# Weighted sums of two attention layers by Strassen's scheme, in groups of two query blocks, with the values projected ahead

## The chip, the core and the metric

The kernel runs on one core of a Trainium2 chip. Five engines work beside each other and meet at semaphores: TensorE (PE in the profile, with its weight loads shown as PEld), VectorE (DVE), ScalarE (ACT), GpSimd (POOL) and SyncE (SP), whose queue issues most of the DMAs; POOL issues the others. The metric is the device time of one execution in microseconds (us).

## What is computed

A stack of four graph layers works on 2708 nodes with 512 features each and one adjacency matrix of 2708 x 2708. After each layer, x becomes the layer norm of x plus the layer's output. The change touches the last two layers, which are attention over all nodes, in fp32:

```python
def _L2_gnn_ref(x, adj, weight, bias, node_w, edge_w):
    node_att = jax.nn.softmax(x @ node_w, axis=0)
    h = x @ edge_w
    e = h @ h.T
    e = jnp.where(adj > 0, e, NEG_BIG)
    edge_att = jax.nn.softmax(e, axis=1)
    combined_att = node_att * edge_att
    support = x @ weight
    output = adj * combined_att @ support
    return output + bias

def _L3_gnn_ref(x, adj_matrix, spatial_matrix, Wq, bq, Wk, bk, Wv, bv):
    query = x @ Wq + bq
    key = x @ Wk + bk
    value = x @ Wv + bv
    scale = 1.0 / jnp.sqrt(jnp.asarray(query.shape[-1], dtype=query.dtype))
    a = query @ key.T * scale
    a = a + adj_matrix + spatial_matrix
    attn = jax.nn.softmax(a, axis=-1)
    return attn @ value
```

In layer 2 the scores `h @ h.T` are symmetric. In layer 3 `adj_matrix` and `spatial_matrix` are both the adjacency. Each layer has two large products: scores (queries by keys) and weighted sums (exponentials by values).

## The kernel before

The nodes are cut into 22 blocks of 128 rows (`BLOCKS`). The last has only 20. A block of queries by a block of keys is a tile of 128 x 128 scores.

Queries are taken in groups of three blocks (`GROUPS`, L1176 to L1182), seven groups, of which the last has four blocks, the short one among them. Keys are taken one block at a time. `softmax_layer` (L1216) builds both layers and returns two functions, and the loop at the end of the kernel calls them: step `t` of `score_step` makes the scores of one key block for one group (`one_score`, L1285), and `sum_step` runs `lag = NT + AHEAD` = 25 steps behind it. So while one group is scored, the one before it is summed. Layer 3's scoring starts 12 steps after layer 2's ends, beside layer 2's last sums.

`one_score` loads the adjacency tile of the step (`load_a`, five buffers), multiplies keys by queries over four chunks of 128 features (L1303), and `score` combines the result with the adjacency: in layer 2 ACT turns the adjacency into a mask (L1650) and DVE applies it (L1651), in layer 3 DVE adds twice the adjacency (L1735). DVE keeps a running maximum (L1351). In layer 2 a score block whose transpose has been made is not made again: the raw scores are copied (L1340), stored in DRAM by POOL, loaded back for the later group and transposed on TensorE (L1295). `key_order` mixes such mirrored steps with the others within a group. The short key block's four feature chunks run packed side by side, and a matmul with `quarters` adds them up (L1337).

When a group is scored, `spread_max` turns its maximum into a row that stands on all partitions (`nmax`). `one_exp`, one step ahead of the sums, subtracts it (DVE, L1401), takes the exponential (ACT, L1402), adds to the row sums (DVE, L1408), and in layer 2 multiplies by a second load of the adjacency (DVE, L1654).

`one_sum` is the weighted sum (L1424). In layer 2 the exponentials of a query block are the weights of the array and 512 value columns stream past, one PSUM bank for each query block, and the four banks are handed round from group to group. In layer 3 the rows of x take the place of the values, and the result is a transposed sum in four banks, one for each 128 features. `end` copies these to SBUF, and `project` multiplies them by `Wv` afterwards (L1532).

`end` also makes the row sums' reciprocals (L1474, L1484). `finish2` scales and adds x (L1660), and later pieces of work, kept in the list `later`, do the layer norm and transpose the new x into the keys of layer 3 (L1195). The loop takes a piece off that list only on odd steps, and none on the last of a group. Layer 3 uses the space of layer 2's values (`sup`) for queries, weights and results.

The order of instructions on an engine follows the program except where a build-time scheduler puts a later instruction in front of one that it takes to be waiting.

Of the kernel before, what the change touches and what calls it, by code (L numbers as in the profile page):

```python
# [29 lines left out]
def gnn_stack_kernel(  # L30
# [1145 lines left out]
    GROUP = 3  # L1176
    lonely = NT % GROUP == 1
    GROUPS = [list(range(g, min(g + GROUP, NT))) for g in range(0, NT - lonely, GROUP)]
    if lonely:
        GROUPS[-1].append(NT - 1)  # L1180
    GSPAN = [(g[0] * P, sum(BLOCKS[it][1] for it in g)) for g in GROUPS]
    GW = max(w for _, w in GSPAN)  # L1182
    GB = max(len(g) for g in GROUPS)

# [5 lines left out]
    def transpose_block(psum, dst, it, copy):  # L1190

        n = BLOCKS[it][1]
        tp = psum.tile([P, C, P], F32, tag="tp", name="tp")
        for c in range(C):
            nc.tensor.transpose(  # L1195
                tp[:, c, :n], xs[:n, it, c * P : (c + 1) * P], ident[:n, :n]
            )
        copy(dst, tp[:, :, :n])
# [15 lines left out]
    AHEAD = 3  # L1214

    def softmax_layer(  # L1216
        att, psum, later, keys, values, query, score, weigh, finish, after=None, sums=None
    ):

        mirror = after is None
        HOME = {it: gi for gi, group in enumerate(GROUPS) for it in group}

        def key_order(gi):

            late = list(range(NFULL // 2)) + [NT - 1] + list(range(NFULL // 2, NFULL))
            if not mirror:

                return late if gi else list(range(NFULL - 1)) + [NT - 1, NFULL - 1]
            early = [jt for jt in late if HOME[jt] < gi]
            late = [jt for jt in late if HOME[jt] >= gi]
            place = {jt: (k + 0.5) / len(early) for k, jt in enumerate(early)}
            place |= {jt: (k + 0.5) / len(late) for k, jt in enumerate(late)}
            return sorted(place, key=place.get)

        kept = {
            (g, gi): dram.tile([GSPAN[gi][1], GSPAN[g][1]], F32, name=f"scores_{g}_{gi}")
            for gi in range(len(GROUPS) if mirror else 0)
# [3 lines left out]
        values4 = []  # L1247

        def last_values():

            t = att.tile([P, F], F32, tag="values4", name="values4", bufs=1)
            for c in range(C):
                nc.gpsimd.dma_start(t[c * Q : c * Q + REST], values[:REST, NT - 1, :])
            values4.append(t)

        def load_a(gi, jt):
            c0, w = GSPAN[gi]
            j0, m = BLOCKS[jt]
            a = att.tile([P, GW], F32, tag="a", name="a_cols", bufs=5)
            if m < P:  # L1260
                nc.vector.memset(a, 0.0)
            for r in range(0, P, P if m == P else Q):
                nc.sync.dma_start(a[r : r + m, :w], adjT[j0 : j0 + m, c0 : c0 + w])
            return a

        def load_kept(gi, jt):

            g = HOME[jt]
            src = kept[g, gi][:, j_in(jt)]
            s = att.tile([P, GB, P], F32, tag="sm", name="s_kept", bufs=3)  # L1270
            full = sum(BLOCKS[it][1] == P for it in GROUPS[gi])
            nc.sync.dma_start(
                s[:, :full, :], src[: full * P].rearrange("(b p) j -> p b j", p=P)
            )
            for b in range(full, len(GROUPS[gi])):
                n = BLOCKS[GROUPS[gi][b]][1]
                nc.sync.dma_start(s[:n, b, :], src[b * P : b * P + n])
            return s

        def j_in(jt):  # L1280

            b = jt - GROUPS[HOME[jt]][0]
            return slice(b * P, b * P + BLOCKS[jt][1])

        def one_score(st, k):  # L1285
            gi, jt = st["gi"], st["order"][k]
            c0, w = GSPAN[gi]
            j0, m = BLOCKS[jt]
            a = load_a(gi, jt)
            ps = psum.tile([P, BANK], F32, tag="ps_s", name="ps_s")  # L1290
            if mirror and HOME[jt] < gi:
                s = load_kept(gi, jt)
                for b, it in enumerate(GROUPS[gi]):
                    n = BLOCKS[it][1]
                    nc.tensor.transpose(  # L1295
                        ps[:, b * P : b * P + n], s[:n, b, :], ident[:n, :n]
                    )
            elif m == P:

                own = mirror and HOME[jt] == gi  # L1300
                b = jt - GROUPS[gi][0] if own else 0
                for c in range(C):
                    nc.tensor.matmul(  # L1303
                        ps[:, b * P : w],
                        keys[:, c, j0 : j0 + P],
                        st["q"][:, c, b * P :],
                        start=(c == 0),
                        stop=(c == C - 1),
                    )
                for o in range(b):  # L1310
                    nc.tensor.transpose(
                        ps[:, o * P : (o + 1) * P],
                        st["own"][o][:, (b - o - 1) * P : (b - o) * P],
                        ident,
                    )
                after_own = (GROUP - b - 1) * P if own else 0
                if after_own:
                    s = att.tile([P, GROUP * P], F32, tag="sraw", name="s_own", bufs=3)
                    nc.scalar.copy(
                        s[:, :after_own], ps[:, (b + 1) * P : (b + 1) * P + after_own]  # L1320
                    )
                    st.setdefault("own", []).append(s)
            else:

                parts = psum.tile([P, BANK], F32, tag="tp", name="ps_parts")
                for c in range(C):
                    nc.tensor.matmul(
                        parts[c * Q : (c + 1) * Q, :w],
                        keys[:, c, j0 : j0 + Q],
                        st["q"][:, c, :],  # L1330
                        start=True,
                        stop=True,
                    )
            e = att.tile([P, GW], F32, tag="e", name="e", bufs=NT + AHEAD + 2)
            if m < P:
                nc.scalar.copy(e[:, :w], parts[:, :w])
                nc.tensor.matmul(ps[:, :w], quarters, e[:, :w], start=True, stop=True)  # L1337
            if mirror and HOME[jt] > gi:
                s = att.tile([P, GROUP * P], F32, tag="sraw", name="s_raw", bufs=3)
                nc.scalar.copy(s[:m, :w], ps[:m, :w])  # L1340
                nc.gpsimd.dma_start(kept[gi, HOME[jt]][j_in(jt), :], s[:m, :w])
# [54 lines left out]
        def one_exp(st, k):  # L1396
# [12 lines left out]
            if weigh:  # L1409
                weigh(e, load_a(gi, jt)[:, :w])  # L1410
# [229 lines left out]
    with (  # L1640
# [41 lines left out]
        def room(first, blocks, *shape):  # L1682
# [3 lines left out]
            for d in shape:  # L1686
                size *= d
# [171 lines left out]
```

## Time and profile before

| what | value |
|---|---|
| median of 3 runs | 3232.13 us (3231.83 to 3232.38) |
| profiled execution, first to last instruction | 3228.0 us |
| layer 2's projections begin to end | about 1465 to 1613 us |
| attention of layers 2 and 3 | about 1613 to 3218 us |
| granted TensorE clock | 0.999 |
| mean DMA rate over the span | 122 GB/s |

The page of a profile lists, for groups of instructions, the line of the kernel, the engine, what is written and read, how many there were, their busy time and mean duration, and what they waited for. An fp32 matmul shows as two records, so that a count of 882 is 441 matmuls. The chain follows the work that ended last back from the end. Busy times of matmuls are partly modelled, so that the distance between starts says more than a mean duration. These groups of the page are of use below:

```profile
L1303 PE MATMUL ps_s<-sup,hT 128*128 128x384 f32 (+1 forms) x1176 | 407.5, 490 | 0.0
L1424 PE MATMUL po<-sup,e 128*128 128x512 f32 x882 | 407.0, 595 | 0.0
L1424 PE MATMUL po<-e,xs 128*128 128x384 f32 (+1 forms) x1176 | 406.1, 489 | 0.0
```

The first is layer 3's scores, the second layer 2's sums, the third layer 3's sums.

### The profile page before, as it was taken

Reading aid. Unit: us, or ns where it says so; the run is one execution under the profiler, and the core shown is the slowest. Engines: PE = TensorE matmul, PEld = TensorE weight load, DVE = VectorE, ACT = ScalarE, POOL = GpSimd, SP = SyncE. Lnnn points to the kernel's source line nnn. Section 1 sums busy time; section 2 is a strip of 40 time slices with the busy share of each in tenths; the row PEclk is TensorE's granted clock in tenths of the full one; section 3 lists DMA queues with packets and bytes.
Section 4 is the critical chain, followed back from the end, with each engine's and each line's share of the span. In section 5 each row is a group of like instructions: output and inputs, shape, how many; then the busy total and the mean of one; then the engine's idle time right before and its main releaser. Section 6 shows DMA issues by size and latency. Waiting matters only on the chain.

```text
span 3228.0 us, 30366 instructions
## 1 busy us (share of the span) xinstructions
PE 3194.0 (99%) x10882; PEld 1714.7 (53%) x10882; DVE 1933.6 (60%) x3166; ACT 1327.7 (41%) x1505; POOL 134.9 (4%) x218
## 2 busy tenths in 40 slices
PE   8999999999999999999999999999999999999999
PEld 5444444544444447875555555554555555555554
DVE  7889987776786784444154677776344342542533
ACT  6898896477867461001142434442011020120211
POOL 1100100000000000000010000000000000000000
PEclk9999999999999999999999999999999999999999
DMA  7867865156546314540054444553211111111100
GB/s 276 307 230 244 292 236 196 45 183 210 182 167 211 139 58 125 143 107 1 0 155 119 129 133 139 146 161 93 75 43 32 44 34 38 43 30 46 34 24 20
DMA packets 175125, 394.81 MB, mean 122 GB/s; under 512 B 21210, under 2 KB 116390, under 8 KB 169150
## 3 DMA queue, kind: packets, MB, share of 16 engines
q1 hardware_dynamic: 158326, 312.84, 32.0%
q0 software_dynamic: 16208, 77.93, 6.3%
q8 instruction: 85, 1.39, 0.2%
q10 hardware_dynamic: 440, 2.10, 0.2%
q14 instruction: 66, 0.54, 0.1%
HBM read 312.69 MB, written 78.52 MB: 121 GB/s over the span
## 4 chain that ended last, share of the span: by engine, by line
PE 79%; DVE 8%; issue 7%; ACT 3%; DMA 2%; POOL 0%; SPq 0%; DVEq 0%; POOLq 0%; ACTq 0%
PE po L1424 24%; PE ps_s L1303 18%; PE po L504 11%; PE ps_nb L1156 7%; PE ps_wide L1205 5%; DVE t L416 3%; PE ps_sup L1601 2%; PE ps_mlp L792 2%; PE ps_o L1532 2%; PE ps_hid L128 2%; ACT t L417 2%; PE ps_dec L923 2%; DVE a L397 1%; ACT t L408 1%; PE ps_s L1295 1%
## 5 line engine op out<-in xcount | busy, mean ns | idle before, releaser
L416 DVE SCALAR_TENSOR_TENSOR t<-t,a 128x2708 f32<-128x2708 f32 (+1 forms) x152 | 450.1, 2974 | 145.3 <-ACT t L408 140.3
L408 ACT ACTIVATE t<-f1b,f2h 128x1354 f32<-128x1354 f32 (+1 forms) x304 | 415.6, 1412 | 44.0 <-PE po L504 34.3
L417 ACT ACTIVATE t<-t 128x2708 f32<-128x2708 f32 (+1 forms) x152 | 373.1, 2456 | 101.5 <-DVE t L416 101.3
L504 PE MATMUL po<-t,xw 128*128 128x452 f32 (+3 forms) x1056 | 407.6, 549 | 4.9 <-ACT t L417 4.4
L1303 PE MATMUL ps_s<-sup,hT 128*128 128x384 f32 (+1 forms) x1176 | 407.5, 490 | 0.0
L1424 PE MATMUL po<-sup,e 128*128 128x512 f32 x882 | 407.0, 595 | 0.0
L1424 PE MATMUL po<-e,xs 128*128 128x384 f32 (+1 forms) x1176 | 406.1, 489 | 0.0
L504 PE MATMUL po<-t,emb 128*128 128x452 f32 (+3 forms) x1056 | 397.7, 545 | 4.0 <-ACT t L417 3.7
L1735 DVE SCALAR_TENSOR_TENSOR e<-a_cols,ps_s 128x384 f32<-128x384 f32 (+1 forms) x154 | 85.5, 555 | 449.2 <-PE ps_s L1303 426.3
L1303 PEld LDWEIGHTS ps_s<-sup,hT 128*128 128x128 f32 x1176 | 221.9, 190 | 164.1 <-issue 14.3
L1424 PEld LDWEIGHTS po<-e,xs 128*128 128x128 f32 x1176 | 222.4, 190 | 160.1 <-issue 6.1
L504 PEld LDWEIGHTS po<-t,xw 128*128 128x128 f32 (+1 forms) x1056 | 188.6, 189 | 212.3 <-issue 191.7
L504 PEld LDWEIGHTS po<-t,emb 128*128 128x128 f32 (+1 forms) x1056 | 193.7, 190 | 201.1 <-issue 189.7
L1424 PEld LDWEIGHTS po<-sup,e 128*128 128x128 f32 x882 | 160.5, 190 | 159.2 <-issue 137.0
L1303 PE MATMUL ps_s<-hT 128*128 128x384 f32 (+5 forms) x672 | 211.1, 461 | 0.9 <-ACT sup L1608 0.7
L1402 ACT ACTIVATE e<-e 128x384 f32<-128x384 f32 (+1 forms) x308 | 151.7, 522 | 117.7 <-DVE e L1401 114.6
L1156 PE MATMUL ps_nb<-hid_hi,at 128*128 128x512 f32 x484 | 185.7, 391 | 0.4 <-DVE at L1148 0.4
L1650 ACT ACTIVATE a_cols<-a_cols,neg_big 128x384 f32<-128x384 f32 (+1 forms) x154 | 94.7, 616 | 219.2 <-DMA a_cols<-in_adjT_dram 183.0
L1156 PE MATMUL ps_nb<-hid_lo,at 128*128 128x512 f32 x462 | 180.2, 390 | 0.0
L108 ACT ACTIVATE ln_rstd<-ln_rstd 128x1 f32<-128x1 f32 (+1 forms) x88 | 17.3, 201 | 389.8 <-DVE ln_rstd L107 389.1
L1401 DVE TENSOR_TENSOR e<-e,nmax 128x384 f32<-128x384 f32 (+1 forms) x308 | 162.6, 550 | 23.3 <-ACT nmax L1394 23.3
L1303 PEld LDWEIGHTS ps_s<-hT 128*128 128x128 f32 x672 | 123.2, 190 | 89.3 <-issue 19.6
(252 smaller groups left out, 3317.7 us busy)
## 6 DMA issues: line engine op xcount, KB each, us to landing
a<-adj_d SPq DMA_DIRECT2D x108, 677.0 KB
a_cols<-in_adjT_dram SPq DMA_DIRECT2D x378, 192.0 KB
a<-in_adjT_dram SPq DMA_DIRECT2D x42, 677.0 KB
adj_d<-a POOLq DMA_DIRECT2D x42, 677.0 KB, 5.9
kept<-t POOLq DMA_DIRECT2D x20, 1354.0 KB, 6.7
t<-kept SPq DMA_DIRECT2D x20, 1354.0 KB
raw<-in_adjT_dram SPq DMA_DIRECT2D x105, 256.0 KB
a_cols<-in_adjT_dram SPq DMA_DIRECT2D x63, 202.0 KB
```

The lines of the kernel that those rows point to most:

```text
L408: tanh = nc.scalar.activation(tv[:, k, :], f1b[k][:n, :w], AF.Tanh, bias=f2h[:n, jt, h : h + 1], scale=0.5,)
L416: step = nc.vector.scalar_tensor_tensor(tv, tv, GUARD, ab, ALU.add, ALU.mult)
L417: exp = nc.scalar.activation(tv, tv, AF.Exp, scale=0.5)
L504: nc.tensor.matmul(po[HB * k + q][:, :qw], values[r : r + n, jt, h * P : (h + 1) * P], t[r : r + n, k, q0 : q0 + qw], start=(place == 0), ...
L1156: nc.tensor.matmul(pos[it][:n], at, half[:, jt, :], start=(jt == 0 and k == 0), stop=(jt == NT - 1),)
L1205: nc.tensor.matmul(ps[:, :width], w(c, o), xt(c), start=(c == 0), stop=(c == C - 1),)
L1303: nc.tensor.matmul(ps[:, b * P : w], keys[:, c, j0 : j0 + P], st["q"][:, c, b * P :], start=(c == 0), stop=(c == C - 1),)
L1401: nc.vector.tensor_tensor(e, e, st["nmax"][:, :w], ALU.add)
L1402: nc.scalar.activation(e, e, AF.Exp)
L1424: nc.tensor.matmul(out, lhsT, rhs, start=(k == 0), stop=(k == NT - 1))
L1650: nc.scalar.activation(a, a, AF.Identity, bias=neg_big[: a.shape[0]], scale=1.0e30)
L1735: nc.vector.scalar_tensor_tensor(e, a, 2.0, ps, ALU.mult, ALU.add)
```

## The change

Queries are taken in groups of two blocks, eleven groups, and keys too: a step is now two query blocks by two key blocks. The last group of both kinds (`REMNANT`) has a full block and the short one. For a pair of full groups, the four products of 2 x 2 blocks (each split into two halves of 256 value columns, so eight of 256 columns) become seven, by Strassen's scheme in Winograd's form. It needs combinations of the values (`S`, and one block of `sup` overwritten), which are made once for each key group, combinations of the exponentials (`T`), which DVE makes in each step, and additions of the seven sums at the end of a group.

In layer 3, the values are projected ahead: layer 2's `later` work multiplies each new block of x by `Wv` and stores it in DRAM. While layer 2's last group is summed, `reload` brings these values into the space of layer 2's values. Rows of x no longer stay in SBUF: they are stored (`x2_d`, `x3_d`) and loaded for each group, and the space they had holds combinations and weights.

The parts of the diff that the text speaks of:

```diff
-    GROUP = 3
+    GROUP = 2
+    GROUPS = [[g, g + 1] for g in range(0, NT, GROUP)]
...
+            a = att.tile([P, GROUP, GW], F32, tag="a", name="a_cols", bufs=4)
+            ps = psum.tile([P, GROUP, GW], F32, tag="ps_s", name="ps_s")
+            e = att.tile([P, GROUP, GW], F32, tag="e", name="e", bufs=LAG + 2)
...
+        def end_exp(st, k):
...
+                    q = e.rearrange("p j (i c) -> p (j i) c", c=P)
+                    sub = lambda d, x, y: nc.vector.tensor_tensor(d, x, y, ALU.subtract)
+                    sub(t[:, 0:2, :], q[:, 1:4:2, :], q[:, 0:2, :])
+                    sub(t[:, 2, :], q[:, 3, :], t[:, 0, :])
+                    sub(t[:, 3, :], q[:, 2, :], t[:, 2, :])
...
+        def row_sums(st):
...
+                for jb in range(GROUP):
+                    nc.tensor.matmul(
+                        pr[:n, b : b + 1],
+                        st["acc"][:, jb, b * P : b * P + n],
+                        ones[:, 0:1],
...
+        def one_sum(st, k):
...
+            product(0, 0, e[:, 0, i1], v0[:, :HF])
+            product(0, 1, e[:, 1, i1], v1[:, :HF])
+            product(2, 0, t[:, 1, :], S[:, g, 2, :])
+            product(2, 1, t[:, 0, :], S[:, g, 0, :])
+            product(1, 0, t[:, 2, :], S[:, g, 1, :])
+            product(1, 1, t[:, 3, :], v1[:, HF:])
+            product(3, 0, e[:, 1, i2], v0[:, HF:])
...
+        def end(st):
...
+                add = lambda d, x, y: nc.vector.tensor_tensor(d, x, y, ALU.add)
+                nc.scalar.copy(at[0][0], po[0][:, 0, :])
+                add(at[1][1], at[0][0], po[1][:, 0, :])
+                add(at[0][0], at[0][0], po[0][:, 1, :])
+                add(at[0][1], at[1][1], po[2][:, 0, :])
+                add(at[1][0], at[1][1], po[2][:, 1, :])
+                add(at[1][1], at[0][1], po[2][:, 1, :])
+                add(at[0][1], at[0][1], po[1][:, 1, :])
+                add(at[1][0], at[1][0], po[3][:, 0, :])
...
+                later.extend(finish(it, parts[b][:n], rs[:n, b : b + 1], r[:n, b, :]))
...
+        def step(t, lag):
+
+            front = t + 1 - lag
+            early = front % NG != 0
+            if early:
+                exp_step(front, begin_exp)
+            if 0 <= t < total:
+                score_step(t)
+            if not early:
+                exp_step(front, begin_exp)
+            exp_step(front, end_exp)
+            if 0 <= t - lag < total:
+                sum_step(t - lag)
+            if 0 <= t < total:
+                score_end(t)
...
+    LAG = NG + 1
...
+        po = [
+            psum.tile([P, GROUP, HF], F32, tag=f"po{b}", name="po", bufs=1) for b in range(4)
+        ]
...
+        def combine(g):
...
+            tt(S[:, g, 0, :], b12, b22, ALU.add)
+            tt(S[:, g, 2, :], b11, b12, ALU.subtract)
+            tt(S[:, g, 1, :], S[:, g, 0, :], b11, ALU.subtract)
+            tt(b12, b21, S[:, g, 1, :], ALU.subtract)
...
+            def project():
+                ps = psum.tile([P, F], F32, tag="tp", name="ps_v")
+                project_rows(ps, hT[:, :, i0 : i0 + n], wv_sb, n)
+                v = att.tile([P, F], F32, tag="T", name="v3", bufs=2)
+                nc.scalar.copy(v[:n], ps[:n])
+                nc.gpsimd.dma_start(v3_d[i0 : i0 + n], v[:n])
+                nc.gpsimd.tensor_tensor(y, y, bv_sb[:n], ALU.add)
+                nc.gpsimd.dma_start(x3_d[i0 : i0 + n], y)
+
+            return [norm, project]
...
+        start3 = steps + 5
+        last2 = steps + LAG - 1
+        nc.sync.dma_start(wv_sb, wv.rearrange("(c p) o -> p c o", p=P))
...
+        for t in range(start3 + steps + LAG):
...
+            if t < steps + LAG:
+                step2(t, LAG)
+            if t >= start3:
+                step3(t - start3, LAG)
...
+            k = t - (last2 - NG + 1)
+            if 0 <= k < NG and order2(REMNANT)[k] != REMNANT:
+                reload(order2(REMNANT)[k])
+            if 2 <= k < NG + 2:
+                g = order2(REMNANT)[k - 2]
+                if g != REMNANT:
+                    combine(g)
-            if later and (k is None or (k % 2 and k < NT - 1)):
+            if later:
                 later.pop(0)()
```

`NG` is the number of groups, 11, and `HF` half of the 512 value columns. `step` runs one step of scores, the exponentials of the step that is summed next, and one step of sums, `LAG` = 12 steps behind the scores. All groups use the same four banks `po`. Where the short key group or the short query group takes part, the plain four products stay, with the 20 rows packed in four quarters of the array. The row sums now come before the last step's products. The list `later` gives up one piece in every step, from the step in which it was filled.

## The prediction

> **What bounds the kernel now.** I read the page's busy line and its chain first, then the chain in order of time and TensorE's timeline in layers 2 and 3, then the windows of layer 2, then VectorE's groups kept apart by shape.
>
> ```profile
> PE 3194.0 (99%) x10882; PEld 1714.7 (53%) x10882; DVE 1933.6 (60%) x3166; ACT 1327.7 (41%) x1505; POOL 134.9 (4%) x218
> ...
> PE po L1424 24%; PE ps_s L1303 18%; PE po L504 11%; PE ps_nb L1156 7%; PE ps_wide L1205 5%; DVE t L416 3%; PE ps_sup L1601 2%; PE ps_mlp L792 2%; PE ps_o L1532 2%; PE ps_hid L128 2%; ACT t L417 2%; PE ps_dec L923 2%; DVE a L397 1%; ACT t L408 1%; PE ps_s L1295 1%
> ```
>
> TensorE (PE) is busy 99% of the span, and the weighted sums (L1424) are the largest entry of the chain, 24%. A busy PE need not be at its peak, so I take spacing. Two stretches of the chain, then TensorE's timeline (start, duration, records):
>
> ```profile
> 2015.10 2.58 PE po L1424 x6
> 2017.67 2.58 PE ps_s L1303 x8
> ...
> 2369.39 2.58 PE ps_s L1303 x8
> 2371.97 2.58 PE po L1424 x8
> ```
> ```profile
> 2053.62 1.02 PE L1424 MATMUL po<-sup,e 128*128 128x512 f32 x2
> 2054.48 0.81 PE L1303 MATMUL ps_s<-hT 128*128 128x384 f32 x2
> 2055.13 1.88 PE L1424 MATMUL po<-sup,e 128*128 128x512 f32 x4
> ...
> 2067.63 1.89 PE L1303 MATMUL ps_s<-hT 128*128 128x256 f32 x8
> 2069.36 0.27 PE L1311 MATMUL ps_s<-ident,s_own 128*128 128x128 f32 x1
> ```
>
> Each fp32 matmul leaves two records. Three 512-wide products take 2.58 us, four 384-wide ones take 2.58: both 0.43 us for each 256 columns. Four 256-wide matmuls with four different weights take 2069.36-2067.63 = 1.73 us, again 0.43 each. So time goes by columns, without a penalty at 256. The first three lines of the timeline also show that the order on the engine is not the program's: at a group's end scores stand between the products of one step, while VectorE still empties banks.
>
> The reserve of VectorE (DVE) decides the rest. Windows of layer 2, then its groups there:
>
> ```profile
> 1780.00:1880.00 100.00, 100.00 (x319) 51.40 (x318) 63.68 (x144) 41.19 (x76) 7.51 (x14) 1.00 0.43 122
> 1880.00:1980.00 100.00, 100.00 (x326) 52.04 (x324) 71.32 (x166) 38.16 (x73) 5.38 (x10) 1.00 0.47 135
> 1980.00:2080.00 100.00, 99.27 (x330) 51.40 (x328) 76.42 (x172) 48.26 (x87) 3.76 (x7) 1.00 0.52 149
> 2080.00:2200.00 120.00, 120.00 (x396) 60.94 (x395) 88.36 (x192) 45.05 (x79) 1.62 (x3) 1.00 0.58 165
> ```
> ```profile
> L1654 DVE TENSOR_TENSOR e<-e,a_cols 128x384 f32<-128x384 f32 x132 | 72.9, 552 | 82.6 <-DMA a_cols<-in_adjT_dram 82.2
> L1651 DVE SCALAR_TENSOR_TENSOR e<-a_cols,ps_s 128x384 f32<-128x384 f32 x132 | 72.3, 549 | 80.0 <-ACT s_raw L1340 58.2 <-PE ps_s L1295 14.2 <-ACT s_own L1319 7.0
> L1401 DVE TENSOR_TENSOR e<-e,nmax 128x384 f32<-128x384 f32 x132 | 69.8, 546 | 8.5 <-ACT nmax L1394 8.5
> ```
>
> The columns of a window are its length, then PE, PEld, DVE, ACT and POOL busy, clock, DMA share, GB/s. PE has no gap worth naming, DVE climbs from 64% to 76%, as later groups mirror more scores and PE's step shortens. Most of DVE's idle time there is waiting, for adjacency tiles and for the raw copies: DVE is not yet late.
>
> [...] weight loads of 190 ns stand beside matmuls without adding to the 0.43 us. [...] Back to back, the trace starts 384-wide operations 0.468 us apart, 400 ns of columns and 68 fixed. From that spacing my estimates are 0.60 us for 512 columns, 0.34 for 256, 0.20 for 128. [...]
>
> **The change, part by part (PE).** Removed in layer 2: 21x21 full products, 147 steps of 2.58 us = 379; seven packed products of the short key block at 1.06 = 7; the short query block 5.5; its sum 1. Together 393. In layer 3: 126 steps of 2.58 = 325, 21 wider ones of 2.71 (404 columns) = 57, short keys 6, projections after the sums (L1532) 21x3.43 = 72, short rows 2. Together 462. Sum 855.
>
> Added, in each layer: 100 pairs of full groups with seven 256-wide products at 0.43 = 301. The short key group costs four products and one packed set, 1.72+0.56 = 2.3, ten times 23. The short query group the same, 23. Corner and picking matmuls 4.5. Together 351, twice 702. Values projected ahead: 22x3.43 = 75. Sum 777. PE gains 78.
>
> Given back: row sums take two one-column matmuls a block instead of one, at 0.19 us each (six records in 0.56): 22x2x0.19 = 8. Eleven sets of packed scores instead of seven: about 1. Score columns, transposed blocks and query columns stay as many, only cut at 256 instead of 384. Net PE: -68 us.
>
> **DVE and its cover.** In layer 2 a step of four blocks costs five 512-wide operations (mask, maximum, shift, row sum, adjacency), 3.0 us, and the new differences 0.34+2x0.20 = 0.74: 3.74, where 3 blocks cost 2.34 before. Eleven steps: 41. Per group come seven bank additions (2.5), finish (2.1), norms (3.4), maximum (1.1), memsets (0.6), and some 2 us of unavoidable waiting from the group's maximum to its first exponential: 53 us. PE in the group that sums gi and scores g=gi+1: 32.5 for sums, 2.7 for its own scores, 3.44x(9-g) for others, 0.44xg for mirrored ones, 1.2 short keys, 7.9 projections and transposes, 1.5 row sums and maxima. That is 59 at gi=5, 56 at 6, 53 at 7, 50 at 8, 47 at 9 (where DVE's narrow scores leave it 48). So DVE's work is hidden until gi=6 and late from gi=7: 0.3+3.3+1.2 = 5 us. [...] I add 3 us for each of five groups, 15. Loss 20. Ends: 0 if the projections, which now lie in this stage, cover all; 60 at 12 us for each of five groups. In layer 3 a step costs DVE 2.4+0.74 = 3.2 us against PE's 6.4: hidden.
>
> ACT: mask, exponential and raw copy at 512 columns stay below 2.2 us a step, plus two table loads a block: below PE everywhere, nothing. DMA: same bytes of adjacency and kept scores, in rows of 1 KB. The rows of x, the values and the reload add about 25 MB over 1600 us, while the share stands at 0.58 at most. On SP the adjacency loads queue behind the load of rows and of the kept scores, with four tiles of 256 KB where there were five of 192: about the same reach of two steps. I cost it at nothing. If that cover fails, the adjacency multiply on DVE is late, inside the 60.
>
> Between layers four steps have only the narrow sums, 2.2 us of PE each, beside DVE's exponentials, reloaded combinations (4x0.34) and norms, about 3 to 3.5 us. POOL's reloads wait for the PE step that frees the block, with value writes queued behind them. Loss 6, from 0 (query projections fill it) to 15. At the start SP's weight loads wait for the last stores of x, ahead of the first adjacency load: 3, from 0 to 5. At the end copy and picking replace projection: 1.
>
> Sum on the profiled execution: 3228.0-68+20+6+3+1 = 3190. The median stands 4.1 us above that span: **3194**.
>
> **The rivals.** First, DVE friction: bank additions, norms and differences hold each of layer 2's last five groups 8 us longer, as DVE runs at over 95%: 3194+35 = 3229. For it: 76% now, and 60% more DVE time a step for a third more blocks. Against: PE did not lose 1 us at 76%, and 75 us of projections move in.
>
> Second, the other side: **group ends stall PE**. All four banks are now owned by one group, and the first norm's transposes are put right after the group's end. They wait for a copy (0.37), seven additions (2.5), reciprocals and finish (2.1), then statistics, square root with table load and scaling (3.2): 8.2 us. If PE stands in that order, 11 ends of layer 2 cost 8 us each, 88, over my 20: 3194+88 = 3282. It decides from 3.5 us exposed per end beyond what is counted above (68-30 = 38 us of gain left, over 11 ends). For it: the same chain ran 8.6 us at 2053.44, from L1484 to L1195. Against: there PE had scores and other products put in between and idled 0.73.
>
> Third, cover is nearly whole: 3228-68+4+4 = 3168.
>
> **How the numbers follow.** Forecast 0.52 (own range 3172 to 3215), cover whole 0.08, DVE friction 0.16, group ends 0.24. No change means within 0.2%, 6.5 us, about what can be told from a measurement: 3225.7 to 3238.6. Friction is spread over 3215 to 3242, so half is faster, 0.07 the same and 0.01 slower; group ends are slower but for 0.02. Faster 0.68, same 0.09, slower 0.23. The range goes from 3164, all cover and no loss, to 3256, which takes in friction and half of the milder stalls.
>
> **What would show it.** Right: seven 256-wide products in 3.0 us on PE; L1424's successors near 700 us in the two layers; DVE above 90% in layer 2 from gi=6 and near 50% in layer 3; PE gaps of 15 to 35 us in all, in layer 2's last third and at its end. Wrong: products spaced over 0.45 us (weights bound), transposes of a norm after a gap of several us at each group end, or gaps waiting for DMA of adjacency or reloaded values.

## The result, and the profile after

| | before | after |
|---|---|---|
| median | 3233.32 us (12 runs, 3229.07 to 3236.45) | 3233.83 us (12 runs, 3230.47 to 3239.01) |
| profiled execution, first to last instruction | 3228.0 us | 3237.0 us |
| ratio of the times, with its 95% interval | | 1.0002 (0.9994 to 1.001) |

No difference can be measured, where 3194 us was forecast. Of the 9 us between the two profiled spans, 4 lie ahead of layer 2's scores (the first one starts at 1618.1 us where it was at 1613.9), in stages that the change hardly touches. There the changed kernel's profile has 13.7 us at a granted clock of 0.5 (at 358 and 860 us), the other 3.4, and at 0.5 a record takes about twice its time (in layer 2 of the changed kernel 256 columns take 0.427 us there and 0.216 at the full clock), so that half of the difference, by estimate 5 us, can account for the 4. It varies from one execution to the next: in the profiles of all kernels here these stages have between 3.4 and 17.1 us of it. The medians don't show the 9 us; the profiled execution of the changed kernel was the longest of its twelve (3239.01).

The page of the changed kernel, its busy line and its chain:

```profile
PE 3168.8 (98%) x13448; PEld 2138.3 (66%) x13448; DVE 2157.1 (67%) x3782; ACT 1347.2 (42%) x1464; POOL 200.5 (6%) x296
...
PE po L1439 17%; PE ps_s L1300 16%; PE po L504 14%; PE ps_nb L1156 7%; PE ps_wide L1206 4%; PE ps_sup L1619 2%; PE ps_mlp L792 2%; DVE t L416 2%; PE ps_hid L128 2%; PE ps_dec L923 2%; DVE e L1383 1%; ACT t L417 1%; DMA a_cols<-in_adjT_dram 1%; DVE a L397 1%; PE psm L541 1%
```

TensorE's busy time fell by 25 us, while the span did not. In the chain the sums fell from 24% to 17%, and two entries of the attention are new: a VectorE operation (L1383, the shift by the maximum) and a DMA of adjacency columns, 1% each. So the chain now leaves TensorE in the attention stage.

The windows of layer 2, the same four as before and three more to its end (window, PE, PEld, DVE, ACT and POOL busy, clock, DMA share, GB/s):

```profile
1780.00:1880.00 100.00, 99.32 (x485) 82.40 (x482) 69.06 (x154) 33.19 (x55) 11.70 (x16) 1.00 0.46 131
1880.00:1980.00 100.00, 97.10 (x453) 75.50 (x452) 77.44 (x172) 39.74 (x66) 19.90 (x22) 0.98 0.49 145
1980.00:2080.00 100.00, 96.57 (x472) 79.41 (x470) 76.58 (x170) 33.69 (x54) 12.56 (x14) 1.00 0.52 150
2080.00:2200.00 120.00, 111.01 (x533) 87.58 (x534) 94.57 (x211) 45.25 (x73) 17.25 (x19) 0.99 0.55 159
2200.00:2300.00 100.00, 90.54 (x395) 65.20 (x394) 84.83 (x189) 40.23 (x65) 11.84 (x14) 0.93 0.53 151
2300.00:2400.00 100.00, 94.76 (x472) 68.24 (x470) 58.28 (x157) 15.64 (x30) 13.60 (x16) 1.00 0.42 120
2400.00:2460.00 60.00, 56.90 (x253) 44.19 (x253) 36.25 (x76) 12.77 (x24) 8.27 (x13) 1.00 0.25 71
```

Three things are to be seen. TensorE, which was busy for 99 to 100% of the four windows before, idles 0.7 us in the first and then 2.9 to 9.5 us in each hundred. VectorE is never full: 58 to 85%. And the granted clock falls below 1 in three of the seven windows, to 0.93 in the one where TensorE idles most. From 1660 to 2460 us TensorE idles 35.8 us in all, against 1.5 before. After 2460, layer 3 alone, it is busy but for 1.6 us near the end.

What TensorE waited for between 1660 and 2460 us, in the list of its waits (total us, times, the longest):

```profile
PE po L1439 <- DVE e L1716: 13.9, 9, 2.3
PE ps_s L1300 <- ACT s_own L1309: 6.0, 3, 2.1
PE ps_s L1294 <- ACT e L1293: 2.9, 3, 1.9
PE tp_mx L1346 <- DVE mx L1340: 2.0, 1, 2.0
PE tp L1198 <- DVE r L123: 1.8, 4, 0.6
```

The largest is for VectorE's multiply by the second adjacency tile (L1716), nine times in eleven groups; five of them, 1.9 to 2.3 us each, stand at ends of groups, 65 us apart. The transposes of the norm (L1198), which the second rival of the prediction had named, take 1.8 us.

**Where the time went, counted.** A busy TensorE hides slow stretches (from 2212 to 2219 us it is busy 7.00 of 7.00 us at a clock of 0.55), so I took the distance from each of its records to the next, from layer 2's first score to the last record of layer 3, and split it: what the columns cost at 0.2133 us for 256 in one record (at full clock the next record starts 0.2160 us after one of 256 columns and 0.4293 after one of 512 in the kernel before, 0.2159 and 0.4292 in the changed one, means of those without a wait or a step: 0.2133 for the 256 columns between them, and 2.5 to 2.7 ns left over for each record), records of narrow tiles (32 rows or columns and less, packed or with 20 rows) at their whole distance, gaps over 0.3 us, and all smaller excess.

| us | length | columns | narrow | gaps | small excess | records |
|---|---|---|---|---|---|---|
| before | 1607.7 | 1529.4 | 42.1 | 2.5 | 33.6 | 4773 |
| after | 1612.8 | 1441.5 | 61.9 | 40.0 | 69.4 | 7056 |
| difference | +5.1 | -87.9 | +19.8 | +37.5 | +35.8 | +2283 |

(The last column leaves out the narrow tiles' records.) Columns and narrow tiles fell by 87.9-19.8 = 68.1 us. All of it came back: half as gaps, half as small excess. Sorted by size and stage, the small excess is this. In layer 3, where TensorE hardly waits, it grew by 11.1 (13.7 to 24.8): 3 of it because each record costs some 2.5 ns beyond its columns, and 8 in steps of about 0.1 us. In layer 2 it grew by 24.6: 12 in such steps, 2 for the records, and 10 in excesses of 0.15 to 0.3 us. Of these last, 6 are matmuls at half clock; 2.0 of the others stand at transposes (L1273) after which the next record starts 0.15 us late or later. 20.5 us of the stage ran at a granted clock of 0.5, against none before. Since a record takes about twice its time there, I estimate half of that as lost, 10 us; about 2 of it are counted among the gaps, since a record of 512 columns took 0.853 us at half clock, an excess over 0.3 us.

### The profile page after: what moved, and what is told of

Its sections match the earlier page's. It is cut to its first block, busy times and chain, and to the rows that moved or that the text cites. A ratio compares the mean times of both kernels' runs of the same rounds, so it can differ in the third digit from the quotient of the medians.

```text
span 3237.0 us, 36055 instructions
## 1 busy us (share of the span) xinstructions
PE 3168.8 (98%) x13448; PEld 2138.3 (66%) x13448; DVE 2157.1 (67%) x3782; ACT 1347.2 (42%) x1464; POOL 200.5 (6%) x296
## 4 chain that ended last, share of the span: by engine, by line
PE 71%; DVE 11%; issue 10%; DMA 3%; ACT 3%; POOL 1%; SPq 0%; DVEq 0%; POOLq 0%; ACTq 0%
PE po L1439 17%; PE ps_s L1300 16%; PE po L504 14%; PE ps_nb L1156 7%; PE ps_wide L1206 4%; PE ps_sup L1619 2%; PE ps_mlp L792 2%; DVE t L416 2%; PE ps_hid L128 2%; PE ps_dec L923 2%; DVE e L1383 1%; ACT t L417 1%; DMA a_cols<-in_adjT_dram 1%; DVE a L397 1%; PE psm L541 1%
## 5 line engine op out<-in xcount | busy, mean ns | idle before, releaser
L1439 PE MATMUL po<-sup,e 128*128 128x256 f32 (+1 forms) x1512 | 404.0, 387 | 16.7 <-DVE e L1716 13.9
L1300 PE MATMUL ps_s<-q,hT 128*128 128x256 f32 (+1 forms) x1848 | 405.6, 372 | 0.0
L1300 PEld LDWEIGHTS ps_s<-q,hT 128*128 128x128 f32 x1848 | 340.0, 190 | 50.4 <-issue 6.7
L1439 PEld LDWEIGHTS po<-sup,e 128*128 128x128 f32 (+1 forms) x1512 | 263.6, 186 | 74.1 <-issue 21.9
L1439 PE MATMUL po<-held,T 128*128 128x256 f32 x1200 | 300.9, 384 | 1.5 <-DVE T L1405 1.1
L1439 PEld LDWEIGHTS po<-held,T 128*128 128x128 f32 x1200 | 227.8, 192 | 35.2 <-DVE T L1405 2.5
L1300 PE MATMUL ps_s<-hT 128*128 128x256 f32 (+2 forms) x968 | 215.0, 372 | 7.2 <-ACT s_own L1309 6.0
L1384 ACT ACTIVATE e<-e 128x512 f32<-128x512 f32 (+1 forms) x242 | 143.4, 612 | 132.6 <-DVE e L1383 131.9
L1712 ACT ACTIVATE a_cols<-a_cols,neg_big 128x512 f32<-128x512 f32 (+1 forms) x121 | 85.2, 705 | 265.0 <-DMA a_cols<-in_adjT_dram 205.4
L1383 DVE TENSOR_TENSOR e<-e,nmax 128x512 f32<-128x512 f32 (+1 forms) x242 | 154.0, 666 | 18.0 <-ACT nmax L1377 16.6
L1786 ACT ACTIVATE q<-ps_wide,uq 128x256 f32<-128x256 f32 (+1 forms) x44 | 20.5, 466 | 332.9 <-PE ps_wide L1206 332.9
```

The source lines that it names most:

```text
L1300: nc.tensor.matmul(ps[:, jb, i:w], keys[:, c, j : j + P], st["q"][:, c, i:], start=(c == 0), stop=(c == C - 1),)
L1383: nc.vector.tensor_tensor(e, e, nm, ALU.add)
L1384: nc.scalar.activation(e, e, AF.Exp)
L1439: nc.tensor.matmul(po[bank][rows, half, :], lhsT, rhs, start=(k == 0 and half == 0) if first is None else first, stop=last, skip_group_che ...
L1712: nc.scalar.activation(a, a, AF.Identity, bias=neg_big[: a.shape[0]], scale=1.0e30)
```

## The experiments

Each row is the median of 4 to 13 executions of a kernel, with the kernel before run beside it; medians of "before" were 3231.8 to 3233.4 us. All ratios are to the kernel before. Each kernel was traced in one execution.

| run | median us | ratio | interval |
|---|---|---|---|
| e1, plain sums in layer 2 | 3253.81 | 1.0063 | 1.0051 to 1.0076 |
| e2, plain sums in layer 3 | 3282.87 | 1.0157 | 1.0143 to 1.017 |
| e3, changed, no second adjacency | 3216.27 | 0.9951 | 0.9939 to 0.9964 |
| e4, before, no second adjacency | 3233.75 | 1.0005 | 0.9996 to 1.0013 |
| e5, finish later | 3221.79 | 0.9962 | 0.995 to 0.9975 |
| e6, own buffer, own copy later | 3233.24 | 1.0003 | 0.9995 to 1.0011 |
| e7, differences on GpSimd | 3247.03 | 1.0043 | 1.0031 to 1.0056 |
| e8, e5 and e6 together | 3214.19 | 0.9939 | 0.9926 to 0.9951 |
| e9, plain sums in both | 3307.14 | 1.0226 | 1.0212 to 1.024 |
| e10, e8 without the second load | 3206.33 | 0.9918 | 0.9904 to 0.9931 |
| e11, e8 without second load and multiply | 3195.72 | 0.9882 | 0.9869 to 0.9896 |
| e12, only the pops later | 3235.68 | 1.0006 | 0.9998 to 1.0014 |

### e1, e2 and e9: the scheme taken out of one layer or both

The edit, used in layer 2, in layer 3, or in both (the combinations of values are left out there too, and two banks serve each group in turn):

```diff
         def one_sum(st, k):
...
+            if plain:
+                for jb, jt in enumerate(GROUPS[g]):
+                    m = BLOCKS[jt][1]
+                    for b in range(GROUP):
+                        nc.tensor.matmul(
+                            po[2 * (gi % 2) + b].rearrange("p h f -> p (h f)"),
+                            e[:m, jb, b * P : (b + 1) * P],
+                            full[:m, jt, :],
...
+                return
```

> The changed kernel with the plain eight products in layer 2 (512-wide, two banks for each group in turn, no differences T, no bank additions); Strassen stays in layer 3. TensorE work +54 us: 100 pairs of groups by one product of 0.43, and 11 for the short keys, which are no longer packed. Theory A (in layer 2 VectorE and the work that feeds it are late, and TensorE idles and is throttled by what Strassen adds there): the idle time of layer 2 falls from about 35 us to under 8, and the whole is within 15 us of the changed kernel, ratio to the kernel before 0.997 to 1.004. Rival B (the loss of layer 2 comes from steps of two by two blocks, whatever the products): idle stays over 20 us and the whole is 35 to 54 us longer, ratio 1.011 to 1.017.

> The changed kernel with the plain eight products in layer 3 alone; Strassen stays in layer 2. Both theories of layer 2 agree here that TensorE alone sets layer 3, so the 54 us of work come back whole: ratio to the kernel before 1.014 to 1.018, idle of TensorE in layer 3 none. A ratio under 1.008 would say that Strassen gained little in layer 3 and that part of the missing gain is to be looked for there.

> The changed kernel's groups, steps, values ahead and stored rows, with the plain eight products (as four 512-wide ones) in both layers, so the change without Strassen's scheme. Theory A, the two layers' savings are independent: the loss of plain layer 2 (0.0063) and of plain layer 3 (0.0157) add up, 1.020 to 1.024, which is about 71 us for the new arrangement alone and 70 us for the scheme. Rival B, the waits of layer 2 shrink further when TensorE has more work beside them: 1.012 to 1.018. Rival C, the losses are the scheme's own and the arrangement is free: 0.999 to 1.005 plus the extra records, at most 1.008.

Against the changed kernel at 1.0002, e2 is 0.0155 slower, 50 us; e1 only 0.0061, 20 us. Counted as above, plain sums have 54.7 us more work in layer 3 (42.7 in columns, 12.0 in narrow tiles) and 48.8 in layer 2 (42.7 and 6.1). Part of the narrow tiles' share belongs to this variant, which multiplies the short key block without packing it. So layer 3 keeps nearly all that the scheme saves, and layer 2 keeps 20 of 49. In e1 the gaps are 21.5 us where the changed kernel has 40.0, and the small excess 56.2 where it has 69.4: taking the scheme out of layer 2 gives back 32 us of loss, and 21.5 stay. e1 lies between the ranges that its theories gave: layer 2 keeps part of the saving, neither all nor nothing.

e9 is the change without the scheme: 1.0226, in the range of theory A, and the two losses simply add (0.0063+0.0157 = 0.022). This variant of the arrangement (groups and steps of two, values ahead, stored rows) costs 73 us, and the change as a whole wins them back. By the count the 73 are 39 in narrow tiles, 15 in gaps, 23 in small excess, and -2.5 in columns. 19 of the 39 come from the short key block, which this variant alone doesn't pack. So by the count the arrangement as the changed kernel has it costs some 54 us, and the scheme wins about as much; no run shows it.

### e3 and e4: without the second adjacency

Left out in both: the adjacency as a factor after layer 2's softmax, its load and its multiply.

```diff
             masked,
-            times_adj,
+            None,
```

> The changed kernel without the second load of the adjacency in layer 2 and without the multiplication of the exponentials by it (left out: the factor adj in layer 2's weighted sum). It takes 0.6 us of VectorE and one transfer of 256 KB from each of 121 steps and nothing from TensorE. Theory A: layer 2's idle time falls from about 35 us to under 10 and the halved clock with it, whole 40 to 60 us shorter, ratio to the kernel before 0.982 to 0.988. Rival C (group ends stall TensorE by the chain from the sums to the transposes of the norm, 8 us each): that chain is not touched, idle stays over 25 us, ratio 0.996 to 1.001.

> The kernel before with the same left out (second load of the adjacency in layer 2 and the factor adj). All theories: TensorE has no idle time to give back there, ratio 0.998 to 1.001. If it falls too, the run of the changed kernel without it says less.

The kernel before doesn't notice (1.0005). The changed kernel gains 0.0051, 16 to 18 us, and its gaps fall from 40.0 to 24.6. The multiply and its load cost nothing before and cost that much now. That lies between the ranges of A and of C: the second adjacency is one cause, and more than half of the gaps stay without it.

### e5 and e12: what stands at a group's end on VectorE

The timeline of the changed kernel at an end of a group, TensorE's idle time ahead of the last line (start, duration, in brackets the wait):

```profile
2077.54 0.75 DVE L1520 TENSOR_TENSOR c<-c,po 128x256 f32<-128x256 f32 x2
...
2078.20 1.41 DVE L1736 SCALAR_TENSOR_TENSOR r<-c,rs,r 128x512 f32<-128x512 f32 x2
...
2079.53 0.68 DVE L114 BATCH_NORM_STATS2 ln_st<-r 128x6 f32<-128x512 f32 x1
2080.13 0.41 DVE L1395 TENSOR_TENSOR acc<-acc,e 128x256 f32<-128x256 f32 x1
...
2080.92 0.67 DVE L1383 TENSOR_TENSOR e<-e,nmax 128x512 f32<-128x512 f32 x1
...
2081.52 0.67 DVE L1716 TENSOR_TENSOR e<-e,a_cols 128x512 f32<-128x512 f32 x1
...
2082.24 1.13 PE L1439 MATMUL po<-sup,e 128*128 128x256 f32 x4 [2.34 <-DVE e L1716]
```

Read it from below. TensorE waits 2.34 us for the multiply of the next group's second step. VectorE has no gap ahead of it: it works off, in order, the last bank additions (L1520), the finish of the group that ended (L1736), the first piece of its norm (L114), and only then the exponentials that TensorE needs next. VectorE takes one after the other, and TensorE's next products need neither the finish nor the norm. The edit puts the finish into the list of later work and takes nothing from the list in a group's first two steps while layer 2 is scored:

```diff
-                later.extend(finish(it, parts[b][:n], rs[:n, b : b + 1], r[:n, b, :]))
+                args = (it, parts[b][:n], rs[:n, b : b + 1], r[:n, b, :])
+                if gi == REMNANT:
+                    later.extend(finish(*args))
+                else:
+                    def begin(args=args):
+                        later[:0] = finish(*args)
+                    later.append(begin)
...
-            if later:
+            if later and not (t < steps and t % NG in (0, 1)):
```

> The changed kernel with the finish of a group (scale and add x, then norm and projection) put off: the finish becomes pieces of the list `later`, and in layer 2 no piece is taken in the step in which a group ends nor in the next. The bank additions stay where they are. Theory D (the jam of VectorE at a group's end, additions, finish and statistics in one queue ahead of the next group's exponentials, makes TensorE wait for the adjacency multiply, 13.9 us in nine waits[...]): these waits fall under 5 us, idle time of layer 2 from 35 to about 22, whole 12 to 22 us shorter, ratio to the kernel before 0.993 to 0.997. Rival E (what is late is the steady step, VectorE's operations and the adjacency loads): the waits only move, ratio 0.999 to 1.002.

e12 has the second hunk alone:

> The changed kernel; only the pieces of later work are not taken in the first two steps of a group while layer 2 is scored, and the finish stays where it is. If the finish standing ahead of the next group's multiply is what e5 relieved: 0.999 to 1.001. If the norm's pieces are: 0.995 to 0.998, as e5's 0.9962.

e5 gains 0.0040 on the changed kernel, 12 to 13 us, in the range of theory D, without a change of any engine's work. The wait shown above falls from 13.9 us to 3.8. The list of e5's waits begins:

```profile
PE tp L1198 <- DVE r L123: 4.8, 5, 2.6
PE tp_mx L1346 <- DVE mx L1340: 4.5, 4, 2.0
PE po L1439 <- DVE e L1724: 3.8, 6, 0.9
```

(L1724 is the multiply there.) e12 gains nothing: the wait for the multiply falls to 8.9 us and that of the norm's transposes rises from 1.8 to 6.1. So the place of the finish in VectorE's order is needed for e5's gain. Whether it is enough without the pieces held back isn't shown: the finish moved alone wasn't run.

### e6: a buffer and a bank

Layer 3's values get a buffer of their own, so that the differences on VectorE don't wait for their store (5.3 us of such waits in the changed kernel), and the copy of a group's own scores (L1309, ACT) is made after both key blocks' matmuls, so that TensorE doesn't wait to write beside it:

```diff
-                    if own and jb == 0 and g != REMNANT:
+                    if own and jb == 1:
                         s = att.tile([P, GROUP, GW], F32, tag="x", name="s_own", bufs=4)
                         nc.scalar.copy(s[:, 0, :P], ps[:, 0, P:])
-                    elif own and jb == 1:
                         nc.tensor.transpose(ps[:, 1, :P], s[:, 0, :P], ident)
...
-                v = att.tile([P, F], F32, tag="T", name="v3", bufs=2)
+                v = att.tile([P, F], F32, tag="v3", name="v3", bufs=1)
```

> Two edits on the changed kernel: the projected values get a buffer of their own instead of one of the two of T, and a group's own scores are copied after both key blocks' matmuls, so that the second block's matmuls no longer wait for ACT's read of the same bank. VectorE waits for T's buffers 20 us in layer 2 (14.9 for TensorE, 5.3 for the store of values), TensorE waits 6.0 us for own copies in three waits. If these waits cost time by themselves: 5 to 10 us shorter, ratio 0.996 to 0.999. If TensorE's order and VectorE's queue absorb them: ratio 0.999 to 1.001.

Nothing is gained (1.0003). The waits of e6 show why:

```profile
PE po L1438 <- DVE e L1715: 13.6, 9, 2.3
PE ps_s L1294 <- ACT e L1293: 6.2, 3, 4.3
PE ps_s L1310 <- ACT s_own L1309: 6.0, 4, 2.6
```

The 6.0 us for the own copy are still there, now ahead of its transpose (L1310), and the packed scores wait 3 us longer. The wait was moved, not removed, and the multiply's is untouched.

### e7: two of the three differences on GpSimd

If VectorE's amount of work were the bound, taking 0.40 us a step off it (two of 0.202) should help.

```diff
-                    sub(t[:, 2, :], q[:, 3, :], t[:, 0, :])
-                    sub(t[:, 3, :], q[:, 2, :], t[:, 2, :])
+                    nc.gpsimd.tensor_tensor(t[:, 2, :], q[:, 3, :], t[:, 0, :], ALU.subtract)
+                    nc.gpsimd.tensor_tensor(t[:, 3, :], q[:, 2, :], t[:, 2, :], ALU.subtract)
```

> The changed kernel with two of the three differences T of each step computed by POOL in both layers: takes 0.40 us of 3.74 from VectorE in each step of layer 2, 44 us over the layer, and puts two POOL operations into the chain of the step. Rival E (the steady step of VectorE is late): 8 to 20 us shorter, ratio 0.994 to 0.998. Theory D: the step is not what is late, and POOL's slower operations come after the exponential, so ratio 0.999 to 1.006.

It is slower, 1.0043, as theory D allowed. The groups of GpSimd by line show the price (count, busy, mean ns, idle before):

```profile
L1407 POOL TENSOR_TENSOR T<-e,T 128x128 f32<-128x128 f32 x103 | 62.8, 610 | 273.7 <-DVE T L1405 243.0 <-PE ps_s L1273 18.9 <-DVE mx L1325 7.8
L1408 POOL TENSOR_TENSOR T<-e,T 128x128 f32<-128x128 f32 x103 | 59.9, 582 | 7.6
```

The two take 1.2 us after each other, and TensorE waits 10.1 us for them in layer 2, while its wait for the multiply hardly falls (12.2 us). It takes work off VectorE without taking away the queue at the group's end, and puts a longer chain behind the exponentials. Since it does both at once, it says that this exchange loses, not that less work on VectorE is worth nothing.

### e8, e10 and e11: all together, and what is left

e8 has the edits of e5 and e6. e10 is e8 where the multiply uses the exponentials themselves in place of a second load:

```diff
-                weigh(e[:, :, :w], load_a(gi, g)[:, :, :w])
+                weigh(e[:, :, :w], e[:, :, :w])
```

and e11 is e8 with the edit of e3.

> The edits of the finish put off, of the own buffer for values and of the own scores' copy together. If the three causes stand side by side, their gains add: idle time of layer 2 under 18 us, half clock under 7 us, 15 to 30 us shorter, ratio 0.991 to 0.996. If one late queue stands behind all of them, no more than the best of the single ones.

> The kernel with all edits of e8, where layer 2's exponentials are multiplied by themselves in place of a second load of the adjacency: the multiply stays on VectorE, the loads and their waits go. Left out: the adjacency as a factor after the softmax. Theory F, the feed of the second load is what is left of the waits: 0.987 to 0.991 of the kernel before, and within 0.001 of the kernel that leaves out the multiply too. Theory V, VectorE's own time is what is left: 0.993 to 0.995, no better than e8's 0.9939.

> As the run before, and the multiply itself left out too (the adjacency as a factor after the softmax). Theory F: 0.987 to 0.991, within 0.001 of the run before. Theory V: 0.986 to 0.991, lower than the run before by at least 0.003.

e8 computes all that the reference does and is faster than both kernels: 0.9939, some 20 us. Layer 2's windows from 2080 us, to be held against the same rows above:

```profile
2080.00:2200.00 120.00, 116.02 (x570) 90.46 (x564) 101.85 (x229) 49.08 (x77) 21.51 (x19) 1.00 0.57 165
2200.00:2300.00 100.00, 95.35 (x437) 71.30 (x438) 83.54 (x198) 38.31 (x61) 11.43 (x12) 0.98 0.54 157
```

TensorE is 116.0 and 95.4 busy where it was 111.0 and 90.5, VectorE does more in the first of them, and the clock, 0.99 and 0.93 there, is 1.00 and 0.98. From 1660 to 2460 us TensorE idles 20.8 us instead of 35.8, and 6.8 us of the stage run at half clock instead of 20.5. e8's interval only touches that of e5, so whether e6's edits help once the finish is out of the way stays open.

e10 says what the second load costs, its arrival, its traffic and the buffers that it holds together: 0.0021, 7 us, with intervals that overlap. e11 says what the multiply costs VectorE: another 0.0036, 11 to 12 us, with intervals apart. Neither theory is right alone: the first step is below V's range and just outside F's, the second as V had it. In e11 14.5 us of gaps remain.

## Why the prediction was wrong, point by point

The profiled executions, term by term, from the count above (us):

| term | forecast | measured |
|---|---|---|
| TensorE's work, row sums among it | -68 | -61 |
| gaps | +30 | +35 |
| half clock | 0 | +10 |
| excess of records, without the row sums | 0 | +21 |
| stages ahead of layer 2's scores | 0 | +4 |
| sum | -38 | +9 |

Gaps and small excess are 73.3 us together in the count; half clock (the estimate above) and the row sums (7.0) are taken out of them here. The +9 is that of these two executions; the medians are 0.5 apart.

**The work on TensorE** was nearly right. The count's -68.1 equals the forecast by luck: the forecast's -68 has 8 us of row sums in it, which the count puts under small excess (7.0 us). With them it is -61. The missing 7 lie in the narrow tiles: the forty packed sets of the short blocks took 0.8 us each on average, waits included, where 0.56 was put. The full products were right: seven start 3.0 us before what follows them, as forecast, and scores of a step take 3.45. Layer 3, in the timeline of TensorE:

```profile
2801.58 1.03 PE L1439 MATMUL po<-sup,e 128*128 128x256 f32 x4
2802.44 1.46 PE L1439 MATMUL po<-held,T 128*128 128x256 f32 x6
2803.74 0.59 PE L1439 MATMUL po<-sup,T 128*128 128x256 f32 x2
2804.17 0.59 PE L1439 MATMUL po<-sup,e 128*128 128x256 f32 x2
2804.60 3.62 PE L1300 MATMUL ps_s<-q,hT 128*128 128x256 f32 x16
```

The fourteen records from 2801.58 to 2804.60 are the seven products: 3.02 us, 0.43 each. The row sums rose by 7.0 us (8.5 to 15.5), forecast 8.

**Layer 3 fully hidden** was right: VectorE is busy 424 of 777 us there (55%), TensorE idles 1.6 us, and e2 measured the scheme's gain as 50 us.

**VectorE's prices** were right: back to back, operations of 512, 256 and 128 columns start 0.602, 0.332 and 0.202 us apart (medians), forecast 0.60, 0.34 and 0.20. The 384 columns between 128 and 512 take 0.400 us by that, which leaves 0.068 or 0.069 of the 0.468 or 0.469 at 384 columns in the kernel before: the split on which the forecast rests. The table loads of ScalarE take 1.283 us each in both kernels.

**The first step that failed is the loss, "DVE and its cover".** It compared VectorE's sum of work in a group with TensorE's, took the larger as the group's time, found VectorE hidden until the seventh group and late by 5 us, and added 15, an allowance of mine that no trace had shown. Both sums were nearly right. In us, for the groups of layer 2 from one end to the next (start of the copy L1521):

| gi | 5 | 6 | 7 | 8 | 9 |
|---|---|---|---|---|---|
| TensorE, forecast | 59 | 56 | 53 | 50 | 47 |
| TensorE, columns and narrow tiles | 59.8 | 56.3 | 53.3 | 51.8 | 47.9 |
| VectorE busy (forecast 53, 2 of them waiting) | 52.5 | 50.8 | 50.1 | 52.0 | 46.8 |
| the group took | 64.9 | 64.2 | 62.5 | 65.5 | 58.9 |

Each group took longer than either sum. VectorE above 90%, the forecast that follows from the comparison, is wrong: it stays at 85% or less. TensorE idled all the same, 32.0 us from 1660 to 2360 where the step had 20, since the time of a group's end is not the time of the group. The bank additions and the finish were in my sum as amounts (2.5 and 2.1 us), but not in their place, ahead of the next group's multiply. e5 shows that this place, with the later pieces held back too, is worth 12 us with no less work. Amounts count as well where they stand ahead of the products: e11 gains 11 to 12 us by leaving the multiply out, though VectorE isn't full in e10 either (86% busy from 2200 to 2300 us).

**The second is the price of TensorE's time, "time goes by columns, without a penalty at 256", at a full clock.** What records and clock cost beyond columns stood in no term, and it is 31 us, more than the 5 by which the gaps were mis-sized. The paragraphs on the clock and on short records have it in parts.

**"DMA: I cost it at nothing"** was too low: VectorE waits 56.8 us for adjacency tiles before L1716, and e10 puts the price of the load at 7 us (barely resolved). In the kernel before those waits were longer (82.2 us in the prediction's rows) and free, as e4 shows: slack covered them.

**The granted clock** was in no term. Of eleven gaps of 1.6 to 2.35 us in layer 2, five were followed within 1.5 us by a stretch at half clock, six were not. Two gaps of 0.95 and 1.93 us lie at 2206.5 to 2210.1, the clock is halved from 2211.4 to 2218.2, and eight records of the same projection take this, once within the stretch and once 11 us later:

```profile
2214.53 5.54 PE L128 MATMUL ps_v<-held,hT 128*128 128x512 f32 x8
...
2225.97 3.60 PE L128 MATMUL ps_v<-held,hT 128*128 128x512 f32 x8
```

So some 10 us of slow matmuls, by the estimate above, came with 35 us of gaps. That the gaps bring them is not shown: I didn't vary this by itself. Half-clock time in the attention falls with the gaps in e8 (6.8 us) and e11 (3.4), which fits; but e6 has 34.1 us with gaps as in the changed kernel (41.4 and 40.0), e7 20.5 with more of them (48.6), and the stages ahead differ by as much in like code. One trace of each kernel doesn't settle it.

**Short records.** Columns as the only price hold within a run of equal matmuls, nearly. Each record has 2.5 to 2.7 ns beyond its columns in both kernels (by the spacing given with the count), 6 us for 2283 more records. Another 20 us are excesses of about 0.1 us, of which 7 are the row sums that I had foreseen. In layer 3, where no wait blurs them, there are 153 (76 before): 65 at one-column row sums (34), 32 where the tile changes its rows or columns (15), and 56 (27) that I couldn't assign. Most of it comes with the arrangement and not with the scheme: e9, which has no seven products, has 23 us more small excess than the kernel before.

**The small terms.** Between the layers I had 6 us; from 2360 to 2460 us TensorE idles 3.8. The start's 3 us didn't come: TensorE idles 0.66 us ahead of the first score in both kernels.

**The rivals.** "Group ends stall PE" had the place right in part and the waiting instruction wrong: not the norm's transposes (1.8 us) but the next group's products, and some 35 us of gaps in all and not 88. "DVE friction" came nearest in time (3229): it had each of the last five groups 8 us longer, and they took 5 to 14 us longer than TensorE's columns and narrow tiles. But its cause, VectorE at over 95%, isn't there.

In sum, of the gaps, with the slow matmuls that may come with them, the order at the group's ends is worth some 12 us (e5) and the second adjacency's load and multiply some 18 (e11 against e8). The gaps that are left in e11, 14.5 us against 2.5 before, weren't traced to single causes, and no experiment took the 21 us of the records away by themselves.

## What to carry to other kernels

Don't compare engines by their sums over a group: where one engine does both a group's closing work and the next group's opening work, write down its queue at the boundary and put what the critical engine needs first in front. When a scheme cuts large products into smaller ones, charge the arrangement it needs (here some 54 to 73 us) separately from what it saves, count its records and not only their columns, and apply it first where the other engines have slack, as layer 3 had and layer 2 had not. Read the clock after TensorE's gaps as well as their length: five of eleven gaps of 1.6 to 2.35 us were followed by 3.4 or 6.8 us at half clock here, though it is not shown that the gaps caused it.

## What the runs showed of the hardware

- Five of eleven gaps of 1.6 to 2.35 us on TensorE were followed by stretches of 3.4 or 6.8 us at a granted clock of 0.5 (20.5 us in all); the kernel before, with 2.5 us of gaps, had none in the attention stage. In the stages ahead of it, nearly the same code ran 3.4 to 17.1 us at half clock from one execution to another.
- At a granted clock of 0.5, records of 128, 256 and 512 columns start 0.213, 0.427 and 0.853 us before the next one, against 0.109, 0.216 and 0.429 at the full clock.
- Each fp32 matmul record of 256 or 512 columns costs 2.5 to 2.7 ns beyond its columns, and 65 one-column records in layer 3 start about 0.11 us before the next one (7.2 us in all).
- A subtraction of 128 x 128 fp32 takes 0.58 to 0.61 us on GpSimd, where VectorE starts the next one after 0.20. Beside them VectorE's 512-wide shift (L1383) took 739 ns on average in layer 2, against 690 without them.
